# A graph attention layer and a transformer block on one core: a load, two value products, mask steps and one attention step moved to other places in a hand-written order

## The chip, the cores and the metric

The kernel runs on one core of a Trainium2 chip. The core has a matrix engine (TensorE, PE in the profile, with its weight loads shown apart as PEld), a vector engine (VectorE, DVE), an engine for activations and copies (ScalarE, ACT), a general engine (GpSimd, POOL), and a sequencer that mostly issues DMAs (SyncE, SP). ScalarE and GpSimd can issue DMAs too. Each engine runs its own instructions in its own program order and waits for the others by semaphores. The metric is device microseconds of one execution, lower is better.

## The reference, cut to what matters

There are 64 batches of 64 tokens with 256 features, a conditioning vector of 256 for each batch, and an adjacency tensor of 64 x 64 x 64 x 11 integers. All is fp32.

The first layer is a graph attention. For each token `self = [x, q] W_self + b_self`, where the conditioning part `q` is zeroed for tokens whose features sum to zero. Then, for two directions `d` (the adjacency and its transpose), 16 heads of width 16 attend to the first 20 tokens of the batch:

```
A    = adj or its transpose, first 20 columns      # (batch, 64, 20, 11)
aff  = where(A.sum(-1) > 0, qh . kh / 4, -9e15) + (A @ w_bias + b_bias)
out += einsum(softmax(aff), self[:, :20]) through Wout + bout
x    = x + relu(self + out of d = 0 + out of d = 1)
```

The second layer is a transformer block with adaptive norms. Six vectors for each batch come from `silu(cond) Wt + bt`: shift, scale and gate for the attention and for the MLP.

```
h = norm(x) * g1 + be1, scaled and shifted;  x = x + gate * (attention(h) Wproj + bproj)     # 16 heads, 64 x 64 scores
h = norm(x) * g2 + be2, scaled and shifted;  x = x + gate * (gelu(h W1 + b1) W2 + b2)         # 256 -> 1024 -> 256
```

## The kernel before, in words

**Tiling.** The 64 batches are cut into nine groups: 4, seven times 8, and 4 batches (`NB`), so 256 or 512 tokens each. Features lie on the partitions (`xT`, `sfT`, `hT`), 512 tokens on the free axis. Softmax works on tiles of 128 tokens (two batches): four tiles in a group of 8, two in a group of 4.

**Three groups in flight.** In `period(g)` the block attention of group g, the graph attention of group g + 1, the MLP of group g - 1 and the first products of group g + 2 are woven together. A period is a run of `slot`s, one for each tile. A slot issues the attention scores of a block tile `E` and a graph tile `C` (`block_scores` L618, `graph_scores` L458), turns and applies the weights of the tiles of the slot before (`block_turned`, `block_attended`, `graph_turned`, `graph_output`), and runs the softmax steps of the new ones (`block_exp` L629 to L635, `block_sums`, `block_weights` L643, `graph_masked` L469 and L474, `graph_exp` L479 to L481, `graph_normal` L488). At named points (`p`, `f0`, `f1`, `d0`, ...) it calls `fill`, which issues pieces of other work that `period` lists in a table for each slot. Between periods stands `boundary(g)`: it ends the last tiles of the period before, adds the attention's projection (`block_proj`), normalizes group g's second half for its block and group g - 1 for its MLP (`norm_tokens`, `norm_stats`, `normed`, `modulated`), and makes queries, keys and values. `start()` opens the pipeline with groups 0 and 1 and two slots; `finish()` closes it.

**What sets the order.** The order of every engine is that of the Python calls: the program is scheduled by hand (`tc.manual_schedule()`, L71). The framework adds semaphore waits for data and for the reuse of buffers. Three kinds of reuse matter here:

- PSUM. Four single banks `s0` to `s3` are handed out in turn by `bank(name)` (L89); one that is held (`py` of the MLP, `pz` of groups 0 to 2) leaves the turn until it is given back. Two pairs, `pa` and `pb`, hold the scores of a slot and then the attended values (`pao`) and outputs (`po`). A matmul into a bank waits until its previous content was read.
- One ScalarE queue does the exponentials, the gelus, and most reads of PSUM (`qT`, `kT`, `qk`, `v1`, `pT`, `wT`, `aoT`). A change between gelu and exponential costs a table load.
- DMAs. SP's queue takes most loads, all stores, and two small round trips through DRAM: `vd` to `vblk` (`graph_v`, `graph_v_spread`), and `nzd` to `nzb` (`nonzero_rows`, L293 and L294), which spreads one flag per token over all partitions; `self_cond` (L315) on GpSimd reads it. ScalarE's queue takes three loads at the start: `condT`, `w_self_q`, `vec`. [...]

**Names that the change touches.** `vec` (L140) holds all bias vectors and norm weights in 48 columns; `col(name, c)` is one of them. `mask_step(g, i)` (L338) makes the masks of a group on VectorE in seven steps: counts (0 and 3), products with `w_bias` (1 and 4), sums (2 and 5), and `keep` and `term` (6). `graph_v(g, 0)` is a product of 128 rows with `Wout` (L371), its bias addition (L373) and a store. `block_v(g, j2)` (L583) makes the values of half a group: four matmuls into one bank, and four ScalarE copies into `v1[j2]` (L595). `block_qk(g, i, c)` makes queries (i = 0) or keys (i = 1), `graph_q(g, d, c)` the queries of the graph. `normed(key)` (L548) subtracts the mean and multiplies by the reciprocal deviation, which GpSimd computes by a power (L546).

**The end.** In `finish` the last group's MLP has its second output half in two steps of 128 tokens (L1223 to L1232), each with a store of its own. Both write one bank, `py`.

Of the kernel before, what the change touches and what calls it, by code (L numbers as in the profile page):

```python
# [9 lines left out]
F32 = mybir.dt.float32  # L10
# [36 lines left out]
def graph_attention_then_dit_block(  # L47
# [48 lines left out]
    def pair(which, name):  # L96
        return ps.tile([P, 2, 512], F32, tag=which, name=name)
# [32 lines left out]
    def load_w(name, src, k, n, eng):  # L130
        t = wpool.tile([P, k, n], F32, tag=name, name=name)
        eng.dma_start(t, src.rearrange("(k p) n -> p k n", p=P))
        return t

    condT = const.tile([P, 2, B], F32, name="condT")
    nc.scalar.dma_start(condT, cond_t.rearrange("(c p) b -> p c b", p=P))
    load_xT(0)
    w_self_q = unit("w_self_q").rearrange("p (k n) -> p k n", k=2)
    nc.scalar.dma_start(w_self_q, w_self[D : 2 * D].rearrange("(k p) n -> p k n", p=P))
    vec = const.tile([P, NCOL], F32, name="vec")  # L140
    nc.scalar.dma_start(vec, vecs)
    w_self_sb = load_w("w_self", w_self[0:D], 2, D, nc.sync)
    wk_sb = [load_w(f"wk{d}", wk[d], 2, D, nc.sync) for d in range(2)]
    load_adj(0)
# [424 lines left out]
    def new_hT(name):  # L569
        return gp.tile([P, 2, GT], F32, tag=name, name=name)  # L570
# [245 lines left out]
    def boundary(g, before):  # L816

        Eb, Cb = before
        e_on, c_on, a_on, m_on = g < NG, g + 1 < NG, g + 2 < NG, g >= 2
        G, A = groups[g] if e_on else None, groups[g - 1]  # L820
        if c_on:
            graph_k(g + 1, 0)
        if m_on and c_on:
            mlp_gated(g - 2, 1)
        if c_on:
            graph_v(g + 1, 1)
            for i in (3, 1, 2, 4) if g == 1 else range(0 if g == 2 else 4, 7):
                mask_step(g + 1, i)
        if m_on and c_on:
            mlp_out(g - 2, 1)  # L830
        block_turned(Eb)
        if g == 1:
            graph_q(2, 0, 0)
        for t in Cb:
            graph_turned(t)
        if not c_on:
            mlp_down(g - 2, 1, *range(4))
        if c_on and g > 1:
            graph_q(g + 1, 0, 0)
        block_attended(Eb, pair("pa", "pao")[:, 0])  # L840
        for t in Cb:
            graph_output(t, pair("pb", "po")[:, 0])
        if g == 1:
            mask_step(2, 5)
            mask_step(2, 6)
            time_added(4)
        if c_on:
            graph_v_spread(g + 1)
            graph_q(g + 1, 0, 1)
        if a_on:  # L850
            load_x(g + 2)
            load_xT(g + 2)
            load_adj(g + 2)
        K = [Tile() for _ in range(A.nt // 2)]
        if g == NG - 2:
            pair_proj(g - 1, 0)
            norm_tokens(G, G.xT, 1)
            norm_stats(G)
            normed(G)
            pair_product(g - 1, 1)  # L860
            graph_q(g + 1, 1, 0)
            norm_tokens(K[0], A.xT, 0)
            pair_gated(g - 1, 1)
            modulated(G, G.hT, 1, amp1, off1, g)
            pair_added(g - 1, 1)
            graph_q(g + 1, 1, 1)
            graph_k(g + 1, 1)
            norm_stats(K[0])
        else:
            if Cb:  # L870
                norm_tokens(G, G.xT, 1)
                norm_stats(G)
            block_proj(g - 1, 0)
            if Cb:
                normed(G)
            block_proj(g - 1, 1)
            if c_on:
                graph_q(g + 1, 1, 0)
            if g == 1:
                graph_q(2, 1, 1)  # L880
            if Cb:
                modulated(G, G.hT, 1, amp1, off1, g)
            if not c_on:
                mlp_down(g - 2, 1, 4, 5)
            if c_on:
                graph_k(g + 1, 1)
            for j2, k in enumerate(K):
                norm_tokens(k, A.xT, j2)
                norm_stats(k)
        if c_on:  # L890
            graph_keys(g + 1, 0)
        if e_on:
            block_qk(g, 1, 0)
            if g == NG - 2:
                norm_tokens(K[1], A.xT, 1)
                norm_stats(K[1])
            block_qk(g, 1, 1)
            block_keys(g, 0)
        for k in K:
            normed(k)  # L900
        A.h2T = new_hT("h2T") if c_on else gp.tile([P, 2, GT], F32, tag="h2b", name="h2T")
        modulated(K[0], A.h2T, 0, amp2, off2, g - 1)
        if not c_on:
            mlp_down(g - 2, 1, 6, 7)
        if e_on:
            block_qk(g, 0, 0)
        if len(K) > 1:
            modulated(K[1], A.h2T, 1, amp2, off2, g - 1)
        if e_on:
            block_qk(g, 0, 1)  # L910
        if c_on and g not in (1, NG - 2):
            graph_q(g + 1, 1, 1)
        if not c_on:
            mlp_gated(g - 2, 1)
            mlp_out(g - 2, 1)
        if a_on:
            nonzero_rows(g + 2)
# [26 lines left out]
    def period(g):  # L944
# [8 lines left out]
            return [(mlp_down, m, c) + ms] if not late or c == 0 else []  # L953

        def masks(*steps):
            return [(mask_step, a, i) for i in steps] if g > 1 and a < NG else []

        def ahead(f, *args):
            return [(f, a) + args] if a < NG else []
# [20 lines left out]
        else:  # L980
            fills = [
                {
                    "f1": [(block_v, g, 0), (block_v, g, 1)],
                    "d0": masks(0),
                    "d2": masks(1) + ahead(self_cond, 0) + ahead(self_cond, 1),
                    "f3": up(0, 1, 2, 3),
                },
                {
# [2 lines left out]
                    "d0": ahead(self_features, 0),  # L991
                    "f2b": ahead(self_product, 1),
                    "d1": ahead(self_features, 1),
                    "d2": masks(2, 3),
                    "f3": up(4, 5),
                },
                {
                    "f0": down(0, 2, 3),
                    "f1": down(0, 4, 5),
                    "f2": ahead(graph_v, 0),  # L1000
                    "f3": up(6, 7),
                },
                {
# [16 lines left out]
    def start():  # L1020
# [74 lines left out]
        for t in t1:  # L1095
# [30 lines left out]
            },  # L1126
            {
                "f1": [(half_normed, 1, 1)],
                "d0b": [(half_normed, 1, 2)],
                "f2": [(graph_v, 2, 0)],  # L1130
                "f2b": [(time_product, 4), (time_product, 5), (time_sum, 4), (time_sum, 5)],
                "f3": [(half_normed, 1, 3)],
            },
# [3 lines left out]
    def finish(before):  # L1137
# [5 lines left out]
        E3 = block_scores(m, 3, [pair("pa", "sca"), pair("pb", "scb")])  # L1143
        block_turned(before[0])
        half_normed(z, 2)
        block_exp(E3)
        mlp_down(l, 0, 6, 7)
        block_attended(before[0], bank("pao"))
        mlp_gated(l, 0)
        mlp_out(l, 0)  # L1150
        half_normed(z, 3)
# [67 lines left out]
                mlp_down(z, 0, i - 1)  # L1219
        mlp_gated(z, 0)  # L1220
        mlp_out(z, 0)
        py, y = bank("py"), two.tile([P, GT], F32, tag="tq", name="y")
        for j in range(2):  # L1223
            t = ts(j, P)
            for i in range(8):
                nc.tensor.matmul(py[:, t], w2_sb[:, i, P : 2 * P], Z.u[i][:, t], start=(i == 0), stop=(i == 7))
            nc.vector.scalar_tensor_tensor(
                y[:, t].rearrange("p (b n) -> p b n", n=N), py[:, t].rearrange("p (b n) -> p b n", n=N), col("b2", 1),
                gate[:, 3, ds(Z.b0 + 2 * j, 2)].unsqueeze(2).to_broadcast([P, 2, N]), ALU.add, ALU.mult,
            )  # L1230
            nc.vector.tensor_tensor(Z.xT[:, 1, t], Z.xT[:, 1, t], y[:, t], ALU.add)
            nc.sync.dma_start(out[P : 2 * P, ds(Z.t0 + j * P, P)], Z.xT[:, 1, t])  # L1232
# [65 lines left out]
```

## Time and profile before

| What | Value |
|---|---|
| median of 3 runs | 682.79 us (682.67 to 682.88) |
| profiled execution, its own time | 687.03 us |
| its span | 685.3 us |
| PE busy | 662.1 us, 97% |
| DVE, ACT, POOL busy | 468.2, 354.6, 371.8 us |
| chain that ended last | PE 82%, DVE 8%, DMA 3%, ACT 3%, POOL 2% |
| mean granted clock | 0.993 |

Times in the profile are microseconds from the start of the span. An instruction row reads: start, duration, engine, line, operation, output<-inputs, shape, count, and in brackets how long the engine had been idle before it and what ended the idle time. L745 is line 745 of the kernel. A row with a count may span small gaps between its instructions. The ends of matmuls are modelled. The boundaries of the program lie at about 78 (boundary 1), 147 (boundary 2), 229, 308, 387, 466 and 544 (boundary 7), and `finish` starts at about 604.

### The profile page before, as it was taken

To read this page: it belongs to the slowest core of one execution; us is meant where nothing else is said; L and a number is where in the kernel's file an instruction comes from. 1 tells how busy PE (TensorE), PEld (TensorE's weight loads), DVE (VectorE), ACT (ScalarE), POOL (GpSimd) and SP (SyncE) were. 2 spreads that over 40 slices of the span, in tenths; PEclk is the share of its full clock that TensorE was granted. 3 is DMA by queue.
4 is the path that set the end of the run, shared out by engine and by line. 5 is a ranking of instruction groups with operands and counts; after the bars stand their busy time and mean duration, and the time that the engine had idled before them with its cause. 6 is when DMAs were issued, how large, how long until landed. Compare 5 with 4: busy or idle time off the path is not lost.

```text
span 685.3 us, 15453 instructions
## 1 busy us (share of the span) xinstructions
PE 662.1 (97%) x6422; PEld 407.6 (59%) x6422; DVE 468.2 (68%) x859; ACT 354.6 (52%) x627; POOL 371.8 (54%) x371
## 2 busy tenths in 40 slices
PE   7999998998999999999999999999999999989997
PEld 6666656674555555556555655555655665556556
DVE  4788976796786677876876767776776865665221
ACT  2355536663566437654476436653377535844411
POOL 5646445764675476554584556745666556444320
PEclk8999999999999999999999999999999999999999
DMA  9426040004000230004000141003000000000000
GB/s 281 150 72 191 21 133 17 10 23 140 13 5 18 64 106 16 4 30 154 1 17 16 37 135 17 2 32 96 1 10 11 24 20 1 3 16 1 17 15 32
DMA packets 34526, 33.42 MB, mean 49 GB/s; under 512 B 5624, under 2 KB 28344, under 8 KB 34456
## 3 DMA queue, kind: packets, MB, share of 16 engines
q1 hardware_dynamic: 33496, 31.74, 14.6%
q8 instruction: 51, 0.84, 0.6%
q0 software_dynamic: 272, 0.33, 0.3%
q10 hardware_dynamic: 688, 0.35, 0.2%
q14 instruction: 19, 0.16, 0.1%
HBM read 25.59 MB, written 6.83 MB: 47 GB/s over the span
## 4 chain that ended last, share of the span: by engine, by line
PE 82%; DVE 8%; DMA 3%; ACT 3%; POOL 2%; issue 1%; ACTq 0%; DVEq 0%; SPq 0%; POOLq 0%
PE py L745 15%; PE pu L735 15%; PE pqT L422 8%; PE pqk L580 7%; PE pv L588 4%; PE ppT L654 4%; PE pwT L496 3%; PE pk L407 3%; PE pproj L690 3%; PE pf L324 3%; PE po L514 2%; PE pv L371 2%; PE pao L665 2%; PE sca L618 2%; PE phT L560 2%; PE pxT L533 2%
## 5 line engine op out<-in xcount | busy, mean ns | idle before, releaser
L745 PE MATMUL py<-u,w 128*128 128x512 f32 (+1 forms) x272 | 119.8, 568 | 2.7 <-ACT aoT L675 2.5
L735 PE MATMUL pu<-h2T,w 128*128 128x512 f32 (+1 forms) x256 | 108.8, 570 | 1.8 <-ACT v L595 1.3
L643 POOL TENSOR_TENSOR pr<-pr,sm 128x1024 f32<-128x1024 f32 x32 | 60.9, 1902 | 69.7 <-DVE sm L642 50.1
L474 POOL TENSOR_TENSOR w<-w,term 128x640 f32<-128x640 f32 x32 | 49.4, 1547 | 76.3 <-DVE w L469 40.3
L735 PEld LDWEIGHTS pu<-h2T,w 128*128 128x128 f32 x256 | 47.7, 190 | 49.4 <-issue 42.8
L745 PEld LDWEIGHTS py<-u,w 128*128 128x128 f32 x272 | 48.3, 192 | 39.3 <-issue 33.0
L422 PE MATMUL pqT<-sfT,wq 128*128 128x512 f32 (+1 forms) x144 | 62.4, 565 | 0.3 <-DVE y L713 0.3
L737 ACT ACTIVATE u<-pu,vec 128x512 f32<-128x512 f32 (+1 forms) x72 | 43.3, 639 | 35.1 <-PE pu L735 34.8
L580 PE MATMUL pqk<-hT,wqkv 128*128 128x512 f32 (+1 forms) x144 | 59.7, 550 | 0.5 <-POOL hT L567 0.4
L629 DVE TENSOR_REDUCE mx<-sca 128x8 f32<-128x512 f32 x32 | 22.1, 690 | 51.8 <-PE sca L458 50.4
L639 DVE TENSOR_REDUCE sm<-pr 128x16 f32<-128x1024 f32 x32 | 38.9, 1217 | 21.4 <-ACT pr L635 20.7
L481 ACT ACTIVATE w<-w 128x640 f32<-128x640 f32 x32 | 23.5, 736 | 55.2 <-DVE w L480 54.2
L423 ACT ACTIVATE qT<-pqT,vec 128x512 f32<-128x512 f32 (+1 forms) x36 | 23.0, 639 | 51.6 <-PE pqT L422 51.4
L635 ACT ACTIVATE pr<-pr 128x1024 f32<-128x1024 f32 x32 | 33.8, 1057 | 30.0 <-DVE pr L631 29.7
L581 ACT ACTIVATE qk<-pqk,vec 128x512 f32<-128x512 f32 (+1 forms) x36 | 23.0, 639 | 47.7 <-PE pqk L580 47.7
L657 ACT COPY pT<-ppT 128x512 f32<-128x512 f32 x64 | 34.4, 590 | 24.9 <-PE ppT L654 24.8
L542 DVE BATCH_NORM_STATS2 st<-xn 128x6 f32<-128x256 f32 x64 | 26.1, 408 | 30.7 <-ACT xn L535 30.7
L546 POOL TENSOR_TENSOR rstd<-rstd,mhalf 128x2 f32<-128x2 f32 x32 | 23.3, 727 | 41.9 <-DVE rstd L545 41.0
L488 POOL TENSOR_TENSOR w<-w,sm 128x640 f32<-128x640 f32 x32 | 44.1, 1381 | 2.9 <-DVE sm L487 2.7
L525 POOL TENSOR_TENSOR xT<-xT,sfT 128x256 f32<-128x256 f32 x32 | 23.3, 727 | 36.0 <-ACT sfT L524 30.8
L551 DVE TENSOR_SCALAR xn<-xn,mv,rstd 128x256 f32<-128x256 f32 x64 | 36.4, 609 | 8.3 <-POOL rstd L546 8.3
L500 ACT COPY wT<-pwT 80x512 f32<-80x512 f32 x64 | 33.9, 581 | 13.1 <-PE pwT L496 13.0
(148 smaller groups left out, 1433.0 us busy)
## 6 DMA issues: line engine op xcount, KB each, us to landing
xT<-in_x_t SPq DMA_DIRECT2D x7, 512.0 KB
out<-xT SPq DMA_DIRECT2D x14, 256.0 KB
a_d<-in_adj SPq DMA_DIRECT2D x7, 440.0 KB
a_d<-in_adj_t SPq DMA_DIRECT2D x7, 440.0 KB
x_g<-in_x SPq DMA_DIRECT2D x5, 512.0 KB
vblk<-vd SPq DMA_DIRECT2D x28, 80.0 KB
w<-in_w SPq DMA_DIRECT2D x2, 1024.0 KB
vd<-v_sb SPq DMA_DIRECT2D x7, 256.0 KB
```

What stands on the lines that cost most here:

```text
L422: nc.tensor.matmul(pq, wq_sb[d][:, k, ts(c, P)], G.sfT[:, k, :], start=(k == 0), stop=(k == 1))
L474: nc.gpsimd.tensor_tensor(t.w, t.w, G.term[:, :, j, :].unsqueeze(1).to_broadcast([P, H, 2, M]), ALU.add)
L488: nc.gpsimd.tensor_tensor(wf, wf, sm.unsqueeze(2).to_broadcast([P, 2 * H, M]), ALU.mult)
L500: nc.scalar.copy(t.wT[:, ts(q4, 4), :], pt[0 : 4 * M, :].rearrange("p (i t) -> p i t", i=4))
L551: nc.vector.tensor_scalar(key.xn[:, i, :], key.xn[:, i, :], key.mv[:, i, 0:1], key.rstd[:, i : i + 1], ALU.subtract, ALU.mult,)
L580: nc.tensor.matmul(pp, wqkv_sb[:, k, ds(i * D + c * P, P)], G.hT[:, k, 0 : G.T], start=(k == 0), stop=(k == 1))
L639: nc.vector.tensor_reduce(t.sm, t.pr, AX.X, ALU.add)
L643: nc.gpsimd.tensor_tensor(t.pr, t.pr, t.sm.unsqueeze(2).to_broadcast([P, H, N]), ALU.mult)
L657: nc.scalar.copy(t.pT[:, ts(q4, 4), :], pt.rearrange("p (i t) -> p i t", i=4))
L735: nc.tensor.matmul(pu, w1_sb[:, k, ts(m, P)], G.h2T[:, k, 0 : G.T], start=(k == 0), stop=(k == 1))
L737: nc.scalar.activation(G.u[m], pu, AF.Gelu, bias=col("b1", m))
L745: nc.tensor.matmul(G.py, w2_sb[:, m, ts(c, P)], G.u[m], start=(m == 0), stop=(m == 7))
```

## The change

Seven edits, in program order:

1. `vec` is loaded first on ScalarE's queue; `condT` and `w_self_q` follow.
2. In the start's second slot `graph_v(2, 0)` moves from point `f2` (behind `block_attended`) to `d0b` (ahead of it and of the reciprocal in `block_weights`).
3. In boundaries 1 and 7 `block_v(g, 0)` is issued at the end of the boundary and no longer in the first slot's `f1`. In boundary 1 `block_qk(1, 0, 0)` also moves ahead of `modulated`.
4. The masks of group 3, which boundary 2 made in one run, are spread: steps 0 and 3 go to the ends of slots 1 and 2 of period 1, steps 1, 2 and 4 stay in boundary 2, steps 5 and 6 go behind `graph_output`. In the same boundary `graph_q(3, 0, 0)` is issued ahead of `graph_turned`, as boundary 1 had it.
5. In boundary 7 `normed(K[0])` runs before the statistics of `K[1]`.
6. In `finish`, `block_attended` of the tile before is issued ahead of `block_exp(E3)`.
7. The last output half uses two banks, one for each step.

```diff
+    vec = const.tile([P, NCOL], F32, name="vec")
+    nc.scalar.dma_start(vec, vecs)
     condT = const.tile([P, 2, B], F32, name="condT")
     nc.scalar.dma_start(condT, cond_t.rearrange("(c p) b -> p c b", p=P))
     load_xT(0)
     w_self_q = unit("w_self_q").rearrange("p (k n) -> p k n", k=2)
     nc.scalar.dma_start(w_self_q, w_self[D : 2 * D].rearrange("(k p) n -> p k n", p=P))
-    vec = const.tile([P, NCOL], F32, name="vec")
-    nc.scalar.dma_start(vec, vecs)
...
             graph_v(g + 1, 1)
-            for i in (3, 1, 2, 4) if g == 1 else range(0 if g == 2 else 4, 7):
+            for i in {1: (3, 1, 2, 4), 2: (1, 2, 4)}.get(g, (4, 5, 6)):
                 mask_step(g + 1, i)
...
         block_turned(Eb)
-        if g == 1:
-            graph_q(2, 0, 0)
+        if g <= 2:
+            graph_q(g + 1, 0, 0)
         for t in Cb:
             graph_turned(t)
...
-        if c_on and g > 1:
+        if c_on and g > 2:
             graph_q(g + 1, 0, 0)
         block_attended(Eb, pair("pa", "pao")[:, 0])
         for t in Cb:
             graph_output(t, pair("pb", "po")[:, 0])
+        if g <= 2:
+            mask_step(g + 1, 5)
+            mask_step(g + 1, 6)
         if g == 1:
-            mask_step(2, 5)
-            mask_step(2, 6)
             time_added(4)
...
             if g == NG - 2:
                 norm_tokens(K[1], A.xT, 1)
+                normed(K[0])
                 norm_stats(K[1])
...
-        for k in K:
+        for k in K[1:] if g == NG - 2 else K:
             normed(k)
+        if g == 1:
+            block_qk(g, 0, 0)
...
         modulated(K[0], A.h2T, 0, amp2, off2, g - 1)
...
-        if e_on:
+        if e_on and g > 1:
             block_qk(g, 0, 0)
...
         if e_on:
             block_qk(g, 0, 1)
+        if g in (1, NG - 2):
+            block_v(g, 0)
...
         def masks(*steps):
-            return [(mask_step, a, i) for i in steps] if g > 1 and a < NG else []
+            return [(mask_step, a, i) for i in steps] if a < NG else []
...
-                    "f1": [(block_v, g, 0), (block_v, g, 1)],
-                    "d0": masks(0),
-                    "d2": masks(1) + ahead(self_cond, 0) + ahead(self_cond, 1),
+                    "f1": [(block_v, g, i) for i in range(1 if g in (1, NG - 2) else 0, 2)],
+                    "d0": masks(0) if g > 1 else [],
+                    "d2": (masks(1) if g > 1 else []) + ahead(self_cond, 0) + ahead(self_cond, 1),
...
-                    "d2": masks(2, 3),
+                    "d2": masks(2, 3) if g > 1 else masks(0),
...
                     "f2": ahead(graph_v, 0),
+                    "d2": masks(3) if g == 1 else [],
...
                 "f1": [(half_normed, 1, 1)],
-                "d0b": [(half_normed, 1, 2)],
-                "f2": [(graph_v, 2, 0)],
+                "d0b": [(half_normed, 1, 2), (graph_v, 2, 0)],
...
         half_normed(z, 2)
-        block_exp(E3)
         mlp_down(l, 0, 6, 7)
         block_attended(before[0], bank("pao"))
+        block_exp(E3)
         mlp_gated(l, 0)
...
-        py, y = bank("py"), two.tile([P, GT], F32, tag="tq", name="y")
+        py, y = [bank("py") for _ in range(2)], two.tile([P, GT], F32, tag="tq", name="y")
         for j in range(2):
             t = ts(j, P)
             for i in range(8):
-                nc.tensor.matmul(py[:, t], w2_sb[:, i, P : 2 * P], Z.u[i][:, t], start=(i == 0), stop=(i == 7))
+                nc.tensor.matmul(py[j][:, 0:P], w2_sb[:, i, P : 2 * P], Z.u[i][:, t], start=(i == 0), stop=(i == 7))
             nc.vector.scalar_tensor_tensor(
-                y[:, t].rearrange("p (b n) -> p b n", n=N), py[:, t].rearrange("p (b n) -> p b n", n=N), col("b2", 1),
+                y[:, t].rearrange("p (b n) -> p b n", n=N), py[j][:, 0:P].rearrange("p (b n) -> p b n", n=N), col("b2", 1),
                 gate[:, 3, ds(Z.b0 + 2 * j, 2)].unsqueeze(2).to_broadcast([P, 2, N]), ALU.add, ALU.mult,
             )
```

## The prediction

> **What bounds the kernel now.** I read the page first, then busy time by stretch, TensorE's waits, and the chain that ended last. From the page:
>
> ```profile
> PE 662.1 (97%) x6422; PEld 407.6 (59%) x6422; DVE 468.2 (68%) x859; ACT 354.6 (52%) x627; POOL 371.8 (54%) x371
> ```
>
> TensorE is the bound. What an edit can win is TensorE's 23 us of idle time, and time in which its clock was down. Both sit in few places, as ten-microsecond stretches show (start and end, length, busy time of PE, PEld, DVE, ACT, POOL, granted clock, DMA share, GB/s):
>
> ```profile
> 10.00:20.00 10.00, 8.88 (x37) 7.59 (x40) 6.34 (x12) 2.53 (x8) 5.93 (x6) 0.66 1.05 365
> ...
> 110.00:120.00 10.00, 8.53 (x98) 6.08 (x97) 6.98 (x12) 8.62 (x17) 6.49 (x6) 1.00 0.08 28
> ...
> 150.00:160.00 10.00, 7.82 (x90) 4.38 (x89) 7.36 (x12) 4.79 (x10) 3.91 (x4) 1.00 0.43 125
> ...
> 560.00:570.00 10.00, 8.62 (x89) 4.48 (x88) 4.97 (x12) 3.22 (x5) 7.24 (x9) 1.00 0.01 2
> 610.00:620.00 10.00, 8.13 (x28) 5.27 (x29) 4.33 (x10) 4.40 (x10) 6.84 (x8) 0.83 0.07 26
> ```
>
> The steady periods between 160 and 500 have 10.00 of 10. A mean clock of 0.66 is 6.8 us at half speed, 0.83 is 3.4 us. The chain's pieces (start, length, what) name what each gap waited for:
>
> ```profile
> 1.85 7.80 DMA vec<-in_vecs
> ...
> 102.49 0.57 DVE nz L291
> ...
> 103.07 8.86 DMA nzd<-nz
> ...
> 112.00 5.47 DMA nzb<-nzd
> ...
> 117.53 2.04 POOL tq L315 x2
> ...
> 610.25 1.06 ACT pr L635
> 611.30 0.52 ACT aoT L675 x2
> ...
> 611.87 3.67 PE py L745 x4
> ```
>
> The last row has four 512-column matmul instructions, which take 1.72 elsewhere; 3.67 is the half clock after a wait. The instruction rows give the wait of boundary 2:
>
> ```profile
> 158.38 0.44 PE L533 MATMUL pxT<-ident,xT 128*128 128x128 f32 x2 [1.72 <-POOL xT L525]
> ```
>
> [...] 6.8 and 3.4 us at half speed, each after a gap (TensorE idle 8.46 to 10.64, and 609.3 to 611.87). [...] So aoT waited behind exponential and table load with its operands there since 608.3. [...] ScalarE's queue moved 0.23 MB from 4 to 5 us, then little, and its last two packets between 9 and 10. [...]
>
> **1. vec first.** The packed vectors (24 KB) were third on ScalarE's queue and landed at 9.65; the first self_features (L331) waited 2.34 us for them. Now w_self_q (256 KB) is third, issued at 1.85 instead of 1.34; the SP issue of wout, which waited for vec at 9.67, now waits for w_self_q. The bounds of its landing: 5.6, were it just 0.5 later than its use at 5.57 suggests, and 9.65, vec's own time in that place. From 5 to 6 us all queues moved only 98 GB/s, so I take 6.2. Then pqw at 6.25 (1.05), pf (1.95, the pair overlapping slightly) to 9.05, sfT and kv to 9.9: the main run of pk starts there and not at 11.56, 1.6 earlier. TensorE's gap shrinks to about half a microsecond twice, so I expect no half clock: pk x14 needs at most 2.2 (8 of twice the columns took 1.25) and pqT x16 3.45 (x4 took 0.86), 5.6 in place of 8.39. Scores would be ready at about 15.5 instead of 19.95, but the next VectorE step also needs the masks, whose input landed at 11.4 and which ended at 16.86. So L469 starts at 16.9 and not 21.23. After allowing 0.3 for wq landing late: **-4.0**. Without the clock's part only the 1.6: -1.6. From there on the data chain, not a transfer, sets the order, so the shift carries.
>
> **2. graph_v(2, 0) before block_attended in the start's second slot.** TensorE's wait of 0.92 at 72.41 is filled with pv. But VectorE is busy without a break from 69.4 to 80, and pk at 78.48 waits for v_sb of that same bank. v_sb moves ahead of a reciprocal (0.24): 0.1 gained there; the reciprocal, the POOL weights (pr, 1.90) and ppT behind them come 0.5 later, against 0.4 of slack. **0**, bounds -0.2 and +0.3.
>
> **3. Boundary 1: block_qk(1, 0, 0) before modulated, block_v(1, 0) before the scores.** Gone are the waits 0.38 and 0.23 at phT, 0.46 at the scores, 1.30 at pu (a bank behind ScalarE's copies of v): up to 2.4. But the transpose of h2T now stands behind one more projection on TensorE: 99.14 + 1.72 = 100.86 in place of 100.05 to 100.6. Queued behind it on VectorE are h2T, rs and nz; nz is then 0.7 later, and with it the two DMAs of 14.4 us on SP's queue. POOL waits for nzb at 117.5 with kb, kblk and the additive mask behind it, and ScalarE's exponential, aoT, which frees the score pair for the next block_scores (126.58), and the gelu follow. TensorE would be there 2 us early and wait. The 2.4 are given back, and the chain is 0.7 late: **+0.7**. If that wait brings a half-clock window, up to 1.7 more; I put 0.4 for it: **+0.4**.
>
> **4. Masks of group 3 spread out, and graph_q(3, 0, 0) before graph_turned.** In boundary 2 VectorE ran seven mask steps from 149.4 to 156.7, and sfT (L523), whose po was ready at 154.5, came behind. Two counts (1.06 each) move to the ends of slots 1 and 2 of period 1, where VectorE waits 0.43 + 1.25 and 0.84 for TensorE and for the exponential behind a table load; those hide them, else they cost 1 us each. Before sfT there now stand 3.2 us, which end at 152.7. The query product fills the 0.46 wait of pwT. Then po is done at about 154.0, sfT 154.4, ACT and POOL add 0.4 and 0.75: pxT needs no wait at 155.8 in place of 158.38. Steps 5 and 6 (1.9 us) end at 156.4, before the statistics need xn. 0.46 + 1.72: **-2.2**. Periods 2 to 6 are TensorE-bound, so it carries.
>
> **5. Boundary 7: normed(K[0]) before norm_stats(K[1]), block_v(7, 0) before the scores.** xn was ready to run at 559.9 (POOL's power ended 559.85) but stood behind the second statistics until 562.48. The waits 0.92 (phT) and 0.7 around the scores (0.47 for qk) go; two v copies precede the exponential. TensorE is about 1.8 ahead at 573. In the next slot ScalarE (gelu x4 of 2.63, two copies, table load, exponential, wT) is the tighter chain and keeps 1.3 of it; **-1.1**, between -0.5 and -1.8.
>
> **6. Finish: block_attended before block_exp.** ScalarE's order changes: aoT (0.61) runs at 608.3, before pr is ready at 608.9, so the exponential loses nothing. py starts at 609.3 in place of 611.87, [...]. The next bound is hT (POOL, 611.88): pqk at 611.95 in place of 615.38; then ppT waits for the weights of pr (614.9 on POOL) in place of 617.97; scores at 618.8 in place of 621.68: **-2.9**. With no clock's part it is -1.1.
>
> **7. Last product in two banks.** The second half waited for VectorE's read of the first (0.45, with drain 0.7): **-0.7**.
>
> Sum: -4.0 + 0 + 0.7 + 0.4 - 2.2 - 1.1 - 2.9 - 0.7 = -9.8. The profiled execution took 687.03 (span 685.3) and becomes 677.2. The median of the runs shown is 682.79, 4.2 below; I carry the same difference: **673.0 us**.
>
> **Rivals.**
> *No clock gain.* The 4.2 us between profiled and other executions could be half-clock windows that these don't have; 3.1 and 1.8 in the profile would be about that size. Against it: three runs agree within 0.21. Then parts 1 and 6 give 1.6 and 1.1: the sum is -5.6 or so, less the 0.4 of part 3: **676.8**.
> *Gains stop at a later wait.* The start stays bound by transfers (w_self_q near 8 us, or wq late), or the stall of period 1 grows by two half-clock windows (3.4): parts 1 and 3 together give nothing or lose: **679**.
> *Slower: w_self_q in the last place.* It takes vec's place and has ten times its bytes. Above 7.9 us each microsecond is one lost, and pqw and pf at half clock cost 2.8 more. The other parts give 5.8 in the profile, so from a landing at about 11.4 the kernel is slower: **684** with 12.5. For it: vec's 9.65 there. Against: those were a few packets behind POOL's loads; 240 packets of w_self_q passed in one microsecond.
> *Nothing arrives*: where the windows fall otherwise and period 1 takes the rest: 682.8.
>
> **How the numbers follow.** First case 0.50 (its own range 671 to 675), no clock gain 0.28, stopped gains 0.10, slower 0.04, nothing 0.04, and 0.04 for more than I count (part 3's waits truly won, under 670.5). The range 670.5 to 678.3 holds the first two and a little of the third. Faster by over 0.2% (1.4 us, about what a measurement of this kernel can tell): 0.50 + 0.28 + 0.10 + 0.04 = 0.92; same 0.04; slower 0.04.
>
> **What would show it.** Right: mean clock near 1.00 in the stretches 10 to 20 and 610 to 620; L331 first waits for TensorE, not for vec; no wait at pxT in boundary 2; py behind aoT under 0.5. Part 3: the nzb wait on POOL grows and TensorE waits at the slot-2 scores. Wrong: pqw waiting for w_self_q beyond 8 us, sfT waiting again in boundary 2, or a new slow-clock stretch near 115 to 130.

## The result, and the profile after

The changed kernel takes **682.84 us** (median of 20 executions, 679.0 to 685.03); the kernel before took 683.29 in the same measurement (20 executions, 681.42 to 686.65). The ratio is **0.9984, 95% interval 0.9968 to 0.9999**: 0.5 us shorter by the medians and 1.1 by the ratio, at the edge of what this measurement can tell from no change. 673.0 was forecast. The two profiled executions stand 5 us apart (681.95 after, 687.03 before), and that pair misleads, as the experiments show.

The lines of after that answer to those shown of before. The page's busy time, and the stretches (start and end, length, busy time of PE, PEld, DVE, ACT, POOL, granted clock, DMA share, GB/s):

```profile
PE 660.4 (97%) x6422; PEld 408.0 (60%) x6422; DVE 471.6 (69%) x859; ACT 354.6 (52%) x627; POOL 371.6 (55%) x371
```

```profile
10.00:20.00 10.00, 9.08 (x45) 7.96 (x46) 6.51 (x13) 2.04 (x6) 4.09 (x5) 0.83 1.07 368
...
80.00:90.00 10.00, 10.00 (x117) 7.01 (x116) 8.73 (x15) 4.97 (x12) 5.21 (x5) 0.88 0.15 46
110.00:120.00 10.00, 8.02 (x96) 6.09 (x95) 8.54 (x15) 7.77 (x14) 5.31 (x4) 1.00 0.17 28
150.00:160.00 10.00, 10.00 (x117) 6.26 (x116) 8.82 (x14) 5.49 (x12) 5.70 (x6) 1.00 0.28 70
560.00:570.00 10.00, 9.52 (x93) 5.42 (x92) 5.14 (x12) 4.09 (x9) 6.84 (x9) 1.00 0.01 2
610.00:620.00 10.00, 9.29 (x102) 6.97 (x103) 7.33 (x14) 3.96 (x9) 6.43 (x8) 1.00 0.07 28
```

Boundary 2 (150 to 160), boundary 7 (560 to 570) and the finish (610 to 620) have less idle time, as forecast. The start does not go as forecast: 3.4 us of it are still at half clock, and a half-clock stretch has come at 79 to 82. The chain of waits shows what the start waits for (start, length, what):

```profile
1.81 8.34 DMA w_self_q<-in_w_self
10.15 0.14 issue
10.29 1.63 PE pqw L224 x8
```

The first product of the conditioning, `pqw`, ran at 5.62 before. It now waits for `w_self_q`, which took the third place on ScalarE's queue and lands at 10.15. This is one of the signs that the prediction named for being wrong. L469, forecast for 16.9, starts at 22.27. TensorE's instruction rows at boundary 2 (start, length, what, shape, count; no bracket, so no wait):

```profile
155.04 0.94 PE L514 MATMUL po<-wT,vblk 80*32 80x64 f32 x32
155.92 1.98 PE L422 MATMUL pqT<-sfT,wq 128*128 128x512 f32 x4
157.74 0.60 PE L533 MATMUL pxT<-ident,xT 128*128 128x128 f32 x4
```

`pxT` follows the query product without the 1.72 us of before. And the row on GpSimd where period 1 gets stuck, before and after:

```profile
117.53 2.04 POOL L315 TENSOR_TENSOR tq<-nzb,qwT 128x512 f32<-128x512 f32 x2 [0.53 <-DMA nzb<-nzd]
...
119.41 2.04 POOL L315 TENSOR_TENSOR tq<-nzb,qwT 128x512 f32<-128x512 f32 x2 [1.31 <-DMA nzb<-nzd]
```

The wait for `nzb` grew from 0.53 to 1.31, and the time that boundary 1 wins is given back behind it, as forecast for part 3. Before, `aoT` ran on ScalarE behind the exponential of `pr` (1.06) and the table load ahead of it (1.28, from 608.95). In the chain of the finish after, `py` no longer stands behind `aoT`:

```profile
610.46 1.14 PE pqk L580 x4
611.60 1.91 POOL pr L643
...
617.40 0.27 PE sca L618 x4
```

In this chain the scores came at 621.75 before. As the finish began 1.5 earlier, 2.9 of the difference belong to part 6.

### The profile page after: what moved, and what is told of

It reads as the page before. It is cut to its first block, busy times and chain, and to the rows that moved or that the text cites. A ratio compares the mean times of both kernels' runs of the same rounds, so it can differ in the third digit from the quotient of the medians.

```text
span 680.3 us, 15452 instructions
## 1 busy us (share of the span) xinstructions
PE 660.4 (97%) x6422; PEld 408.0 (60%) x6422; DVE 471.6 (69%) x859; ACT 354.6 (52%) x627; POOL 371.6 (55%) x371
## 4 chain that ended last, share of the span: by engine, by line
PE 83%; DVE 8%; ACT 3%; POOL 2%; issue 2%; DMA 1%; ACTq 0%; POOLq 0%; DVEq 0%
PE py L745 14%; PE pu L735 14%; PE pqT L422 8%; PE pqk L580 8%; PE ppT L654 4%; PE pv L588 4%; PE pwT L496 3%; PE pf L324 3%; PE pproj L690 3%; PE pk L407 3%; PE po L514 3%; PE pv L371 2%; PE pao L665 2%; PE sca L618 2%; PE phT L560 2%; PE pxT L533 2%
## 5 line engine op out<-in xcount | busy, mean ns | idle before, releaser
L745 PE MATMUL py<-u,w 128*128 128x512 f32 (+1 forms) x272 | 118.1, 561 | 0.2 <-ACT u L737 0.2
L422 PE MATMUL pqT<-sfT,wq 128*128 128x512 f32 (+1 forms) x144 | 60.7, 551 | 0.3 <-DVE y L713 0.3
L551 DVE TENSOR_SCALAR xn<-xn,mv,rstd 128x256 f32<-128x256 f32 x64 | 37.9, 633 | 9.7 <-POOL rstd L546 9.7
```

Source lines behind the costliest of these rows:

```text
L422: nc.tensor.matmul(pq, wq_sb[d][:, k, ts(c, P)], G.sfT[:, k, :], start=(k == 0), stop=(k == 1))
L551: nc.vector.tensor_scalar(key.xn[:, i, :], key.xn[:, i, :], key.mv[:, i, 0:1], key.rstd[:, i : i + 1], ALU.subtract, ALU.mult,)
L745: nc.tensor.matmul(G.py, w2_sb[:, m, ts(c, P)], G.u[m], start=(m == 0), stop=(m == 7))
```

## The experiments

Each kernel was timed in turn with the kernel before, on the same chip. A ratio is given with its 95% interval; medians of before moved between 682.2 and 685.0 from chip to chip, so ratios are compared, not times, unless the two kernels were on one chip. A window is a stretch of 3.4 us at half clock: the granted clock was 0.50 from 611.9 to 615.3 in the profile of before, and from 10.6 to 14.1 and 78.9 to 82.3 in that of after. At that length and that clock one of them takes 0.0025 from the mean granted clock of an execution of 683 us, so the clock says, as an estimate, how many windows it had.

### 1. The kernel before once more

> The kernel before, unchanged, to see the granted clock of many of its executions beside their times. Theory W (the change saves time in each stretch, but its usual execution has one or two half-clock windows of 3.4 us more than the usual execution of before, each worth 1.5 to 1.8 us): most executions at a mean clock of 0.995 or 0.997 and 681.5 to 683.5 us, and those at 0.992 at about 685 to 687. Rival L (no more windows than before; the late w_self_q and the second stall simply eat the gains): most executions at 0.992 and about 683, as after.

Measured: 683.54 us (680.61 to 686.47, 14 executions), ratio 1.0009 (0.9993 to 1.0026). The times follow the clock: 680.6 at 0.999 and 1.000, 682.6 to 683.1 at 0.997, 684.0 to 686.5 at 0.994 and 0.995. After had 679.0 to 679.6 at 0.997, 680.7 to 682.4 at 0.994 and 0.995, 682.5 to 683.9 at 0.991 and 0.992. Theory W holds, though at 0.994 and 0.995 before is one to three microseconds longer than it expected: at the same clock after is about 3 us shorter than before, but it usually has about one window more (mean clock 0.9930 against 0.9961). A straight line through the executions of one kernel, of each that has eleven or more, gives 1.4 to 1.9 us for a window.

The profile holds the second finding. TensorE's rows at the start, and a row of all waits (engine, line, what it waited for, total, times, longest):

```profile
9.59 0.45 PE L407 MATMUL pk<-kv,wk 128*128 128x80 f32 x2 [0.36 <-POOL kv L332]
10.53 1.79 PE L407 MATMUL pk<-kv,wk 128*128 128x80 f32 x14 [0.49 <-POOL kv L332]
```

```profile
DVE sfT L331 <- DMA vec<-in_vecs: 0.5, 1, 0.5
```

In the profile that the prediction was made from, `pk` began at 10.64 and its main run at 11.56, after a wait of 2.34 for `vec`. Here the same program waits 0.5 for `vec`, and it has one half-clock window in the start (12.9 to 16.3, on `pqT`) instead of two (11.1 to 18, on `pk` and `pqT`). In five further profiles with the same load order (runs 2, 4, 8, 9 and 10 below) there is no wait for `vec` at all, and the main run of `pk` starts between 10.48 and 10.98. The late `vec` was an exception, not the kernel's usual state.

### 2. After with the old load order

```diff
-    vec = const.tile([P, NCOL], F32, name="vec")
-    nc.scalar.dma_start(vec, vecs)
     condT = const.tile([P, 2, B], F32, name="condT")
     nc.scalar.dma_start(condT, cond_t.rearrange("(c p) b -> p c b", p=P))
...
     nc.scalar.dma_start(w_self_q, w_self[D : 2 * D].rearrange("(k p) n -> p k n", p=P))
+    vec = const.tile([P, NCOL], F32, name="vec")
+    nc.scalar.dma_start(vec, vecs)
```

> After, with the order condT, w_self_q, vec of before (part 1 undone; parts 2 to 7 kept). Theory S (the start is what lost: w_self_q lands 4 to 5 us later, the start ends 1.0 us later in the profiled pair where 4.0 less was forecast): 681.8 us or a little less, 1.0 below after. If parts 4 to 7 give in the median what they give in the profiled pair (2.4 + 1.0 + 2.9 + 0.7) and period 1 gives back 1: 677. Rival L: 683, no different from after. In the trace pqw again starts near 5.6 us.

Measured: 676.8 us (675.88 to 677.9), ratio **0.9911 (0.9894 to 0.9928)**. Undoing part 1 alone takes 0.6% to 0.7% off after. Of the two times expected the 677 came true: the profiled pair had hidden the loss, for there before had the late `vec` and two half-clock windows in the start, and after only one window. `pqw` starts at 6.82, not near 5.6, and `w_self_q` lands 3.5 earlier than in after. TensorE's rows:

```profile
6.82 1.08 PE L224 MATMUL pqw<-condT,w_self_q 128*128 128x64 f32 x8 [1.19 <-DMA w_self_q<-in_w_self]
...
10.64 1.79 PE L407 MATMUL pk<-kv,wk 128*128 128x80 f32 x14 [0.49 <-POOL kv L332]
```

The main run of `pk` is at 10.64 where after has 15.70, and the start's `pv` (L371) is at 17.43 where after has 22.40.

### 3. Before with part 1 alone

```diff
+    vec = const.tile([P, NCOL], F32, name="vec")
+    nc.scalar.dma_start(vec, vecs)
     condT = const.tile([P, 2, B], F32, name="condT")
     nc.scalar.dma_start(condT, cond_t.rearrange("(c p) b -> p c b", p=P))
...
     nc.scalar.dma_start(w_self_q, w_self[D : 2 * D].rearrange("(k p) n -> p k n", p=P))
-    vec = const.tile([P, NCOL], F32, name="vec")
-    nc.scalar.dma_start(vec, vecs)
```

> Before with part 1 alone: vec first on ScalarE's queue, then condT, w_self_q; everything else as before. Theory S: pqw near 10 us, 2.5 to 6 us slower than before (686 to 689 us). The forecast of part 1 was -4.0 (679). Rival (the loss comes only together with the other parts): 682 to 684.

Measured: 688.09 us against 683.09 of before on the same chip, ratio **1.0062 (1.0040 to 1.0083)**: 5.0 us slower by the medians. `pqw` starts at 10.61 after a wait of 3.66 for `w_self_q`. So the loss needs none of the other parts. The stretch from 10 to 20 of this run:

```profile
10.00:20.00 10.00, 8.85 (x39) 7.79 (x40) 5.29 (x11) 1.40 (x5) 2.84 (x4) 0.66 1.07 370
```

Here the start has two half-clock windows, where the six later profiles with the old order (runs 1, 2, 4, 8, 9 and 10) have none or one.

### 4. Before with parts 4 to 7 alone

The edit is the diff of the change without its first three items (boundary 7 keeps `block_v` at its end).

> Before with parts 4 to 7 alone (masks of group 3 spread and graph_q(3,0,0) early, boundary 7, the finish, two banks); loads, graph_v(2,0) and boundary 1 as before. Theory P (these parts are won as forecast: 2.2 + 1.1 + 1.1 to 2.9 + 0.7): 676.4 to 678.2 us against 683.3. Rival L (in the usual execution the gains of the profiled pair are not there): 682 to 683.

Measured: **675.86 us** (675.39 to 679.07), ratio **0.9913 (0.9889 to 0.9936)**. Executions with a clock of 0.999 or 1.000, so without a window, took 675.4 to 675.9; those of before on this chip took 680.6 to 681.7. The difference of their medians, 5.2, stands beside the forecast for these four parts without the clock, 2.2 + 1.1 + 1.1 + 0.7 = 5.1. Two of the stretches:

```profile
560.00:570.00 10.00, 10.00 (x93) 6.31 (x92) 6.31 (x10) 4.81 (x11) 4.60 (x5) 1.00 0.01 2
610.00:620.00 10.00, 9.40 (x130) 6.32 (x129) 6.80 (x14) 3.59 (x8) 5.02 (x5) 1.00 0.01 2
```

Theory P holds. What is left, up to 5.9 by the ratio and 7.2 by the medians, can be clock in part: the means, 0.9982 against 0.9964, are 0.7 windows apart, about 1 us.

### 5. vec early, but on another queue

```diff
-    vec = const.tile([P, NCOL], F32, name="vec")
-    nc.scalar.dma_start(vec, vecs)
     condT = const.tile([P, 2, B], F32, name="condT")
     nc.scalar.dma_start(condT, cond_t.rearrange("(c p) b -> p c b", p=P))
     load_xT(0)
+    vec = const.tile([P, NCOL], F32, name="vec")
+    nc.sync.dma_start(vec, vecs)
```

> After, with vec issued on SyncE's queue behind the first xT, and only condT and w_self_q on ScalarE's (parts 2 to 7 kept). It puts vec early without making w_self_q the third. Theory S: pqw near 5.6 us, L331 first waits for TensorE, the main run of pk at about 10 us; L469 at about 17 to 19 us where before had 21.23; time 676 to 679 us, 2 to 4 below the old order. Rival: vec wins nothing, because the next wait (masks, wq, or w_self behind vec on SyncE's queue) ends at the same time: the same as with the old order within 0.7 us.

Measured: 676.53 us, ratio 0.9909 (0.9891 to 0.9927); with the old order 0.9911. The rival holds: an early `vec` wins nothing that can be told, though `w_self_q` lands earlier too (`pqw` at 6.11). TensorE's rows show what comes next:

```profile
9.73 2.10 PE L407 MATMUL pk<-kv,wk 128*128 128x80 f32 x16 [0.63 <-DMA wk<-in_wk]
12.91 3.69 PE L422 MATMUL pqT<-sfT,wq 128*128 128x256 f32 x16 [1.07 <-DMA wq<-in_wq]
```

`pk` does start 0.9 earlier than with the old order, and then `pqT` waits for `wq`. Its scores come at 16.53 (15.94 in run 2). In run 2 the masks are as late: they end at about 17.5, when L469 starts (17.88 here).

### 6. After with work in TensorE's pause

```diff
         pq = bank("pqw")
+        for _ in range(12):
+            nc.tensor.matmul(pq[:, 0:P], ones, ones, start=True, stop=True)
```

> After with twelve more products of ones (128 x 128) on TensorE ahead of pqw, some 3 us of work that nobody needs, in the pause in which it waits for w_self_q; the bank is overwritten by pqw. Nothing lands earlier. If the clock is most of part 1's loss (theory C: 4 to 5 of 6 us are windows at half speed, 1 to 1.5 is the late landing): 678 to 679.5 us, mean clock 0.997 or more, pk and pqT of the start at 1.8 and 3.7 us. If the late landing itself is the loss (theory D): 682 to 683, as after.

Measured: 679.69 us (678.53 to 680.72), ratio 0.9939 (0.9923 to 0.9955). After, run again on this chip (run 7), had 681.4. The rows and the stretch:

```profile
6.84 2.98 PE L223 MATMUL pqw<-ones 128*128 128x128 f32 x24
10.40 1.07 PE L226 MATMUL pqw<-condT,w_self_q 128*128 128x64 f32 x8 [0.58 <-DMA w_self_q<-in_w_self]
```

```profile
10.00:20.00 10.00, 9.08 (x72) 7.63 (x72) 7.95 (x14) 2.97 (x8) 5.57 (x6) 1.00 1.07 370
```

With the pause filled the granted clock is 1.00 from 0 to 10 us and from 10 to 20, though `w_self_q` lands no earlier (10.27). That took 1.7 us off after by the medians and 2.4 by the ratios. What is left over the old order on this chip (676.96, run 8, which leaves out part 3 too) is 2.7: the late landing itself. Neither theory alone holds; from these differences part 1's loss is estimated as some 2.7 of landing and some 2 of clock, each uncertain by more than a microsecond. The same kernel meets the windows differently from execution to execution: on one chip, 19 executions of before had clocks from 0.994 to 1.000 and times from 680.8 to 684.5.

### 7. After once more

> After, unchanged, for the places of its half-clock windows in another execution. Theory S (w_self_q lands near 10 us in each execution, and TensorE's pause ahead of pqw brings one to three half-clock windows in the first 20 us or soon behind): 682 to 684 us, pqw at 9.5 to 10.5 us, a clock of 0.992 with windows at the start and one where the stall at phT falls. Rival V (the late landing was that one execution's): pqw before 8 us, windows elsewhere.

Measured: 681.4 us (679.84 to 683.16, 11 executions), ratio 0.9974 (0.9960 to 0.9988), clock 0.9935 in the mean. `pqw` at 10.00 after 2.96 of waiting, half-clock windows at 10.4 and 78.7: in the same places as in the first profile. The time is a little under the range of theory S and the clock a little above; otherwise it holds, and the landing at 10 us is no accident.

### 8. Old load order, without part 3 in boundary 1

```diff
-        if g == 1:
-            block_qk(g, 0, 0)
...
-        if e_on and g > 1:
+        if e_on:
             block_qk(g, 0, 0)
...
-        if g in (1, NG - 2):
+        if g == NG - 2:
             block_v(g, 0)
```

(and `block_v(1, 0)` back in `f1`).

> After with the loads of before (part 1 undone) and with boundary 1 of before (part 3 undone for group 1; boundary 7 keeps its part). Parts 2 and 4 to 7 remain. Forecast of part 3: it costs 0.7 without the clock: 676.1 us against 676.8 with it. Rival (part 2 is what costs between 676.8 and the 675.9 of parts 4 to 7 alone): 676.8.

Measured: 676.96 us, ratio 0.9900 (0.9882 to 0.9917), against 0.9911 (0.9894 to 0.9928) with part 3: no difference that these runs can tell. By the traces part 3 costs about a quarter of a microsecond: the run with it (run 2) leads by 0.50 ahead of boundary 1 (`pqk` at 91.74 against 92.24) and by 0.26 behind boundary 2 (`phT` at 157.25 against 157.51). In between it is 2.9 us ahead (scores at 108.39 against 111.28) and then waits 1.82 for the gelu at `ppT`; without part 3 that wait is 0.17.

### 9. Old load order, without part 2

```diff
-                "d0b": [(half_normed, 1, 2), (graph_v, 2, 0)],
+                "d0b": [(half_normed, 1, 2)],
+                "f2": [(graph_v, 2, 0)],
```

> After with the loads of before (part 1 undone) and with graph_v(2, 0) of the start's second slot back at f2 (part 2 undone). Parts 3 to 7 remain. Forecast of part 2: nothing (676.8 us, as with it). Rival: part 2 turns two short waits of TensorE (0.9 at pao, 0.4 at phT) into one of 1.2 at phT and costs some 0.9: 675.9.

Measured: 679.33 us on a chip where before took 684.98, ratio 0.9903 (0.9877 to 0.9930) against 0.9911 with part 2: no difference that can be told. Two traces agree: run 2 (with parts 2 and 3) starts `pv` 0.27 ahead of run 4 (without) and `pqk` of boundary 1 0.04 ahead, so part 2 costs some 0.2. TensorE's short waits became one of 1.2 at `phT`. In both profiles of after a half-clock window begins beside that wait; in run 2, with the same wait, none does.

The profile of this run shows something else, which the prediction had named: a half-clock stretch in period 1. GpSimd waits three times as long for `nzb` as in run 2 (0.97), and TensorE's wait for the scores behind it grows from 0.78 to 2.92:

```profile
117.60 2.04 POOL L315 TENSOR_TENSOR tq<-nzb,qwT 128x512 f32<-128x512 f32 x2 [3.10 <-DMA nzb<-nzd]
126.66 0.49 PE L618 MATMUL sca<-kb,qk 32*64 32x128 f32 x4 [2.92 <-issue]
```

From 126 to 133 the clock is at one half, two windows. The profile of run 11 has the same (3.06, 2.88, 126 to 133), that of run 12 a `nzb` wait of 2.61 and, ahead of its end, one window from 118 to 122. All three have part 3 and ran on one chip, where from the issue of `nzd` to the end of the wait 14.9 to 15.4 us passed; in the profiles with part 3 from the other chips it was 13.0 to 13.6, and period 1 had no window. No profile without part 3 has one there, run 10 on the same chip included, whose `nzb` wait is 0.17. How often it happens is not known: six of the seven executions of run 9 had a clock of 0.997 or 1.000, so one window at most.

### 10. Before with part 6 alone

```diff
-        block_exp(E3)
         mlp_down(l, 0, 6, 7)
         block_attended(before[0], bank("pao"))
+        block_exp(E3)
```

> Before with part 6 alone: in the finish, block_attended of the tile before ahead of block_exp(E3). Forecast: 1.1 us without the clock, 2.9 where the half-clock window at 612 us goes with it. Executions of before without any such window took 680.6 to 681.0: without windows 679.5 to 679.9. If the window at 612 is in most executions of before, the median falls from 683.1 by 2.5 to 2.9 (680.3); if it is in few, by 1.1 (682).

Measured: 681.42 us (20 executions), before 684.98 on the same chip, ratio 0.9955 (0.9940 to 0.9970): **-3.1 us**, between 2.1 and 4.1. Mean clock 0.9984 against 0.9951. That is 1.3 windows fewer in the mean execution. The window at 612 us was not in the first profile alone: the profile of run 1 has it too (610 to 614), that of run 3 does not. So the forecast for this part, -2.9 with the window, was right for most executions, though it was made from one.

### 11 and 12. What makes w_self_q late

Two edits of after: `condT` behind `w_self_q`, and the small broadcasts `wb` and `bb` moved from GpSimd's queue to ScalarE's.

```diff
-    nc.scalar.dma_start(condT, cond_t.rearrange("(c p) b -> p c b", p=P))
...
     nc.scalar.dma_start(w_self_q, w_self[D : 2 * D].rearrange("(k p) n -> p k n", p=P))
+    nc.scalar.dma_start(condT, cond_t.rearrange("(c p) b -> p c b", p=P))
```

```diff
-    nc.gpsimd.dma_start(wb, w_bias.partition_broadcast(P))
+    nc.scalar.dma_start(wb, w_bias.partition_broadcast(P))
     bb = const.tile([P, 1], F32, name="bb")
-    nc.gpsimd.dma_start(bb, b_bias.partition_broadcast(P))
+    nc.scalar.dma_start(bb, b_bias.partition_broadcast(P))
```

> After with ScalarE's queue in the order vec, w_self_q, condT: w_self_q second, condT (64 KB) third. Theory Q (what is third on this queue has its bytes after 4.5 us, when the queues together moved only 70 to 100 GB/s, and lands late whatever it is): pqw still later than 8 us, now behind condT, time 680 to 683. Theory B (it is the size of w_self_q, 256 KB, that makes the third place expensive): condT lands by 7 us, pqw at 6.5 to 7.3, time 676.5 to 677.5.

> After with the two small broadcasts wb and bb on ScalarE's queue behind w_self_q instead of GpSimd's. In the traces of after wb's few packets take 0.4 to 0.6 us each, between 4 and 6.5 us, while all queues together move 70 to 100 GB/s. If these packets hold back w_self_q (theory K): pqw at 7 to 8 us, time 678 to 680. If it is only its place behind vec and condT, or the other broadcasts (bout) on GpSimd's queue: pqw at 9.5 to 10.3 and 681 to 683.

Measured: 682.81 us, ratio 0.9977 (0.9959 to 0.9995), and 683.08, ratio 0.9974 (0.9957 to 0.9990); neither differs from after. `pqw`'s row in the first:

```profile
8.47 1.08 PE L224 MATMUL pqw<-condT,w_self_q 128*128 128x64 f32 x8 [1.56 <-DMA condT<-in_cond_t]
```

Theory Q: here `condT`, third on the queue, lands late (8.33) even with a quarter of the bytes, though 1.8 us earlier than `w_self_q` did. In the second `pqw` starts at 9.27; `wb` on GpSimd's queue is not the cause by itself.

### 13. All broadcasts of GpSimd later

```diff
+    nc.gpsimd.memset(vblk, 0.0)
+    for t in v1:
+        nc.gpsimd.memset(t, 0.0)
     wb = const.tile([P, L], F32, name="wb")
     nc.gpsimd.dma_start(wb, w_bias.partition_broadcast(P))
...
             self_features(0, c)
-        nc.gpsimd.memset(vblk, 0.0)
...
-        for t in v1:
-            nc.gpsimd.memset(t, 0.0)
```

(the tiles `vblk` and `v1` are defined ahead of it; the six other broadcasts follow `wb`.)

> After with all seven broadcasts of GpSimd's queue issued 3.6 us later (the memsets of vblk and v1, which GpSimd does anyway, stand ahead of them); vec still first and w_self_q third on ScalarE's queue. Theory G (between 4.3 and 6 us all queues together move only 70 to 150 GB/s because GpSimd's broadcasts are being set up and moved, and the third load of ScalarE's queue falls into that trough): the trough moves 3.6 us later, w_self_q lands by 6.5 to 7.5 us, pqw by 7.5, time 676.5 to 678. Rival (the trough has another cause, or stands at the same place without GpSimd): pqw still at 9 to 10.5, time as after, 0.997 of before.

Measured: 678.77 us (677.28 to 680.25), ratio **0.9950 (0.9931 to 0.9968)**. From 4 to 6 us the DMA view of after has (total, then by queue: q1 is SP's, q10 ScalarE's, q0 GpSimd's; packets, MB, share of 16 engines):

```profile
DMA packets 375, 0.23 MB, mean 114 GB/s; under 512 B 190, under 2 KB 375, under 8 KB 375
...
q1 hardware_dynamic: 149, 0.14, 22.2%
q0 software_dynamic: 28, 0.00, 18.9%
q10 hardware_dynamic: 198, 0.08, 15.0%
```

and of this run:

```profile
DMA packets 635, 0.54 MB, mean 270 GB/s; under 512 B 131, under 2 KB 635, under 8 KB 635
...
q1 hardware_dynamic: 305, 0.29, 50.0%
q10 hardware_dynamic: 330, 0.25, 42.0%
```

The trough is gone and ScalarE's queue moves three times as much. As packets differ in size, their number is the fairer count: in these two microseconds it is 504 at most in the profiles of the kernels with the broadcasts in their old place, and 635 and 850 in runs 13 and 14, where they are later. `w_self_q` lands at 8.37 and not at 10.15, which lies between theory G (6.5 to 7.5) and its rival (9 to 10.5), and so does the time. So the broadcasts account for 1.8 of the 3.5 us by which it is later than in run 2 (6.68), and for a third to a half of the time lost (0.995 against 0.9974 and 0.9984 of after, of which 0.991 would be all). The rest stays with the third place on the queue; what makes that place late without the broadcasts was not tested, nor why the queues of the other two engines move less than half as much while GpSimd's first packets are on their way.

### 14. Parts 4 to 7, and the broadcasts later

> Parts 4 to 7 alone on before (loads of before) and GpSimd's broadcasts 3.6 us later, as in the run beside it. Parts 4 to 7 alone gave 0.9913 of before. Theory G: w_self_q, wk, adj and wq land earlier, the first 20 us end up to 1 us earlier, few half-clock windows: 0.989 to 0.990 of before. Rival: the broadcasts now collide with adj and wq, which the start waits for last: 0.992 or more.

Measured: **675.05 us** (674.85 to 678.71) against 682.16 of before on the same chip, ratio **0.9911 (0.9887 to 0.9935)**. The ratio lies between the two expectations. Without windows it took 674.9 to 675.1, some 0.6 under run 4 on another chip, and the start's scores come at 15.88 (16.21): a gain of a few tenths, which the interval cannot tell from none. Runs 4 and 14 both beat before by 0.9% and after by 0.6% to 0.7%.

## Why the prediction was wrong, by its steps

**Part 1, forecast -4.0, measured +4.2 to +5.0** (run 3, by the ratio and by the medians; after once more against run 2, 0.0063 or 4.3 us). This step makes 8.2 to 9.0 of the 9 us or so by which the change in time was missed, and it failed three times over.

- *The base.* The wait of 2.34 for `vec` and the half clock behind it were read from one profile, whose execution was 4.2 us longer than the median of the other three. The text noticed the difference and carried it over ("I carry the same difference") instead of asking which of its waits belonged to it. Six other profiles of that load order have a `vec` wait of 0.5 or none. The forecast's -4.0 was the way of L469 from 21.23 to 16.9, less 0.3. With the same load order L469 starts at 17.47, 17.56 and 17.97 in runs 2, 4 and 8, and at 19.56 and 19.68 where a window falls on `pqT` (runs 1 and 9), so that 1.5 to 3.8 of the 4.0 were not there to be won. VectorE's rows of before and, the last one, of run 2:

```profile
9.79 0.48 DVE L331 SCALAR_TENSOR_TENSOR sfT<-pf,vec,tq 128x256 f32<-128x256 f32 x1 [2.34 <-DMA vec<-in_vecs]
...
21.23 0.49 DVE L469 TENSOR_TENSOR w<-sca,keep 128x320 f32<-128x320 f32 x1 [4.37 <-PE sca L458]
...
17.47 0.48 DVE L469 TENSOR_TENSOR w<-sca,keep 128x320 f32<-128x320 f32 x1
```

- *The landing of `w_self_q`.* 6.2 was taken between bounds of 5.6 and 9.65; it was 10.15, 9.87 and 10.47 in three profiles, above both bounds. `pqw` and `pf` then met a half-clock window as well (10.6 to 14.1 in after). The argument against a late landing was that 240 packets of `w_self_q` passed in one microsecond. They did so from 4 to 5 us, just ahead of the trough which the same text had seen ("from 5 to 6 us all queues moved only 98 GB/s"). Behind `vec` and `condT`, `w_self_q` came into the trough: in after, ScalarE's queue moved 148 packets from 4 to 4.5 us and 2 from 4.5 to 5. The rival "w_self_q in the last place" named the place and its price: a microsecond for each above 7.9 and 2.8 for `pqw` and `pf` at half clock, which with 10.15 makes 5.0, where 4.2 to 5.0 were measured. That is luck in part, for between run 2 and after the traces have 3.5 of landing and 1.5 of half clock. It got 4 in 100. It gave the bytes as the reason, where run 11 shows that a quarter of them lands late too; and by its own figures the kernel is slower from a landing at 10.9 (7.9 + 5.8 - 2.8), not 11.4.
- *The ceiling.* Run 5 shows that an early `vec` gives nothing even without a late `w_self_q`: `wq` and the masks end the wait. The 0.3 allowed for `wq` was too little.

**Part 2, forecast 0 (-0.2 to +0.3).** Right in the traces (about +0.2). The new wait of 1.2 at `phT` was not foreseen; beside it after has a half-clock window at 79. It cost about 0.8: after is 4.98 behind run 2 at the start's scores and 5.77 behind it at the first scores of period 1.

**Part 3, forecast +0.7 and +0.4.** The mechanism was right: the gain is there by the scores (2.9 us, run 8) and is given back behind ScalarE's exponential and gelu (a wait of 1.82 at `ppT`), and the wait for `nzb` is longer (1.31 against 0.53). The size was off: about +0.2 in the traces of runs 2 and 8, nothing in the times. The 0.4 put in for a half-clock window stood for something real, as the three profiles under run 9 show, but not for the usual execution.

**Parts 4, 5 and 7, forecast -2.2, -1.1, -0.7.** Right. In the profiled pair after gains 2.35 at boundary 2 (`pproj` at 158.34 against 158.82 after having stood 1.87 behind), 1.0 at boundary 7 and 0.7 at the end; parts 4 to 7 together, with part 6 at its 1.1, gave 5.2 without windows where 5.1 was forecast.

**Part 6, forecast -2.9.** Right: 2.9 in the pair, 3.1 alone. The 1.8 of it that the forecast put down to the clock was its author's estimate; the granted clock from 610 to 620 went from 0.83 to 1.00.

**The sum.** Without part 1 the forecast's parts add to -5.8, and run 2 without part 1 measured -0.89%, 6.1 us. "Nothing arrives" (682.8, 4 in 100) met the number of after by luck, for another reason than it gave: 6.1 gained and the 4.2 (by the ratio) to 5.0 (by the medians) that run 3 measured for part 1 leave 1.1 to 1.9, where the two measurements of after have 1.1 (0.9984) and 1.8 (0.9974).

## What to carry to other kernels

Before a wait in a profile is priced, ask whether it is in the usual execution: a profile longer than the median may have something the others lack, as here the wait of 2.34 for `vec`, which in six other profiles was 0.5 or none. Moving a small load ahead costs the large one behind it its place, here 3.5 us of its landing; ask when that one's bytes will go out, and what else the DMA engines move at that time. The pause of TensorE ahead of `pqw` cost twice, once in waiting (some 2.7 us, estimated from runs 6 and 8) and once in the clock behind it, and work that nobody needs, put into the pause, bought the second part back (1.7 to 2.4 us, run 6).

## What the runs showed of the hardware that was not expected

- A window at half clock (3.4 us) is worth 1.4 to 1.9 us of this kernel's time, and their number differs by three to four between executions of the same program: 20 executions of after had clocks from 0.989 to 0.997, 57 of before on one chip 0.989 to 0.999. The pauses ahead of them were as short as 2.54 (before, 609.3 to 611.87) and, in after, 1.19 (at `phT`), though in run 2 no window followed that one.
- While GpSimd's seven broadcasts start, from 4 to 6 us, all queues of after together moved 114 GB/s; with these broadcasts 3.6 us later the same two microseconds moved 270. GpSimd's own packets took only 18.9% of the 16 engines' time in that trough, and SP's and ScalarE's 22.2% and 15.0%; what held those two back was not shown.
- A load of 24 KB, put ahead of the 64 KB that stood there already, delayed a load of 256 KB on the same queue by 3.5 us, from a landing at 6.68 to 10.15; 1.8 us of that went when GpSimd's broadcasts came later (8.37, run 13).
- A small round trip through DRAM (`nzd`, `nzb`) took 13.0 to 13.6 us in six profiles with part 3 and 14.9 to 15.4 in the profiles of runs 9 to 12, all from one chip; in two of them a wait of 2.9 us on TensorE and two half-clock windows came with it.
